# Turning x and v by transfers alone in a graph-network kernel: the transposes of x leave TensorE, a scale factor leaves the first layer norm, and the prologue is laid out anew

## The chip, the cores and the metric

The kernel runs on one core of a Trainium2 chip. The metric is the time of one execution on the device in microseconds (us); the median of three runs before the change is 2247.48 us (2246.62 to 2248.86). The engines of the core are PE (TensorE, with PEld for its weight loads), DVE (VectorE), ACT (ScalarE), POOL (GpSimd) and SP (SyncE), which here only issues transfers.

## The reference, cut to what matters

There are 64 graphs of N = 256 nodes, with D = 256 features in x and an adjacency matrix `adj` of integers. Two layers follow each other, each with a residual and a layer norm:

```
# layer 0: three rounds of message passing, each followed by a GRU cell
A = (adj != 0); h = x
for i in 0..2:
    a = A^T (h W_i)
    r = sigmoid(a Wir + h Whr + b); z = sigmoid(a Wiz + h Whz + b)
    n = tanh(a Win + bi + r * (h Whn + bh))
    h = (1 - z) * n + z * h
x1 = layernorm(x + h)                  # (v - mean) / sqrt(var + 1e-5), v = x + h

# layer 1: graph attention
Wh = x1 W;  s1 = Wh a1;  s2 = Wh a2
e = leaky_relu(s1[:, None] + s2[None, :], 0.2), and -9e15 where adj <= 0
x2 = layernorm(x1 + softmax(e) Wh)
```

## The kernel before

**Tiles.** Two graphs make a pair (NP = 32 pairs, K = 4 tiles of 128 nodes to a pair). Features lie on the partitions wherever they are contracted: `hT` holds h as [128, 2 halves of D, 512 nodes]. x comes from DRAM with nodes on the partitions, and `to_T` (L265) turns it: four 128x128 transposes on PE for each half of D, L269, and a copy out of PSUM by ACT and DVE in turn (L113, L115).

**Precision.** A product of float32 numbers is made of pieces: `upper` (a rounded high part, ACT, L129), `lower` (the rest, L132) and `cross` (L135, DVE). Weights are cut into pieces once, by `cut_weight`. The aggregation with A takes x or h as `hi` and `lo` (L306, L132). For layer 0 `lo` is made on POOL, for the others on DVE.

**Work of one block (p, i): pair p, layer i.** `front` (L291) turns h where needed (`turn`, L275 for i > 0), makes `hi` and `lo` (`split`, `rest`), aggregates (L340: 16 matmuls of 256 columns, eight for each half of D), and cuts h and the aggregate into pieces. `gates` (L357) runs 72 matmuls of 512 columns (L369) in eight products; each product ends with an evacuation by ACT (L374, L376) and one by DVE (L378). Then come sigmoid and tanh on ACT (L387), and products, differences and sums on POOL (L395, L396 in `blend`; L401; L405); the sum that makes the new h is on DVE (L408).

**Attention of a pair** (`attention`, L442). x in its turned form was put away in DRAM (`stash`, xT) and comes back as `vT`; DVE adds h (L451). `halves` splits v's numbers into their two 16-bit halves (ACT L460, DVE L461), `back` turns the halves by two transposing transfers of 256 KB on SP (L469), `join` brings them together as v with nodes on the partitions (ACT L478, DVE L479). `layer_norm` (L410) takes the statistics (L418, L419), rs = (var + eps)^-0.5 on POOL (L422, L423), and scales v on ACT (L430). `project` (L493) multiplies vT by W and the attention vectors, with the mean taken out of the weights; `spread` scales by rs (L502, L504). Scores, mask, maximum and exponentials follow (L512, L516, L525, L527, L530), the transposes of the exponentials (`weights_T`, L540) and their copy (L558), the product with Wh (`combine`, L548), its sum with v (`add`, L554), the second layer norm, and the store.

**Order.** A planner written in the kernel keeps a heap of steps with due times in ticks. `gates` lets the clock tick as it lays out its products, 12 ticks a block; whatever is due is laid out there, and each engine runs its own instructions in this order. Blocks go round as (T, 0), (T-1, 1), (T-2, 2), so three pairs are under way, and a turn of 36 ticks brings in one pair. The front of a block is laid out one block ahead of its gates, at the paces `LOOSE` (2, 3, 4, 6, 7, 8 for turn, split, rest, aggregate, upper and rest of the aggregate) or `CLOSE`. The attention of a pair begins with its third block's end, t; its steps stand at t+5 to t+72.

**Buffers.** x and adj have one buffer each (tags "x" and "adj"), hT four, A three. `wh` holds v's 16-bit halves and later Wh; `sc` holds the turned halves and later the scores; both have one buffer but in the last two pairs. All transfers in the loop are issued by SP, one after another; an issue that waits holds up all that stand behind it.

**Prologue.** w_hh is loaded and turned by PE (`rows_T`, L213) and cut; then w_ih; `fold` (L226) makes W_i w_ih; then come x and the first block's front.

Of the kernel before, what the change touches and what calls it, by code (L numbers as in the profile page):

```python
# [9 lines left out]
F32 = mybir.dt.float32  # L10
F32R = mybir.dt.float32r
U8 = mybir.dt.uint8
U16 = mybir.dt.uint16
I32 = mybir.dt.int32
AF = mybir.ActivationFunctionType
ALU = mybir.AluOpType
# [10 lines left out]
def kernel(  # L27
# [77 lines left out]
    def bank(name):  # L105
        return psum.tile([P, 512], F32, tag="bank", name=name)
# [53 lines left out]

    loaded, loaded_adj = {}, {}

    def load_x(p):
# [9 lines left out]
    def load_rows(src, tags, eng):  # L173

        ts = []
        for tag, (o0, o1) in zip(tags, ((0, 4), (4, 6))):
            t = work.tile([P, C, GN], F32, tag=tag, name=f"rows_{tag}_{o0}")
            v = t.rearrange("p a b -> p (a b)")[:, :(o1 - o0) * D].rearrange("p (o d) -> p o d", d=D)
            eng.dma_start(v, src[o0 * P:o1 * P].rearrange("(o p) d -> p o d", p=P))
            ts.append((o0, o1, v))  # L180
        return ts

    wh_n = load_rows(w_hh, ("hH", "hL"), nc.sync)
    wi_n = load_rows(w_ih, ("aH", "aL"), nc.scalar)
    w_n = []
    for i, tag in enumerate(("wh", "v", "v")):
# [4 lines left out]
        w_n.append(t)  # L191
    load_x(0)
    load_adj(0)
    make_identity(nc, ident)
    nc.gpsimd.memset(half, -0.5)
    nc.gpsimd.memset(neg, NEG_INF)
    nc.gpsimd.dma_start(bi, b_ih.rearrange("(c p) -> p c", p=P))
# [9 lines left out]

    def rows_T(src, use):
        for c in range(C):
            for o0, o1, t in src:  # L210
                pt = bank("pw")
                for o in range(o1 - o0):
                    nc.tensor.transpose(pt[:, o * P:(o + 1) * P], t[:, o, c * P:(c + 1) * P], ident)  # L213
                use(c, o0 * P, o1 * P, pt[:, :(o1 - o0) * P])

    def square_T(src, name):
        pt = bank("pw")
        for e in range(C):
            for d in range(C):
                nc.tensor.transpose(pt[:, (e * C + d) * P:(e * C + d + 1) * P],  # L220
                                    src[:, d, e * P:(e + 1) * P], ident)
        dst = work.tile([P, K, P], F32, tag="hi1", name=name, bufs=1)
        nc.scalar.copy(flat(dst), pt)
        return dst.rearrange("p k n -> p (k n)").rearrange("p (e d) -> p e d", e=C)

    def fold(i, wT, d):  # L226
        for o0, o1 in ((0, 512), (512, O)):
            pt = bank("pw")
            for e in range(C):
                nc.tensor.matmul(pt[:, :o1 - o0], wT[:, e, d * P:(d + 1) * P], wih(e, o0, o1),  # L230
                                 start=(e == 0), stop=(e == C - 1))
            cut_weight([t[:, d, o0:o1] for t in wc[i]], pt[:, :o1 - o0], f"{i}_{d}_{o0}")
# [32 lines left out]
    def to_T(src, dst, d):  # L265
# [4 lines left out]
        after(1, lambda: evacuate(dst[:, d, :], pt))  # L270

    def from_T(hT, d):
        pt = bank("pt")
        for k in range(K):
            nc.tensor.transpose(pt[:, k * P:(k + 1) * P], hT[:, d, k * P:(k + 1) * P], ident)  # L275
        return pt

    def begin(p):

        s = pairs[p] = Pair()  # L280
        s.x, s.adj = loaded.pop(p), loaded_adj.pop(p)
        s.A = work.tile([P, G, C, N], F32R, tag="A", name=f"A_{p}", bufs=3)
        nc.vector.tensor_scalar(s.A, s.adj, 0.0, None, op0=ALU.not_equal)
        s.hT = work.tile([P, C, GN], F32, tag="hT", name=f"hT_{p}", bufs=4)

# [5 lines left out]
    def front(p, i, t, pace):  # L291
# [4 lines left out]
        def turn(d):  # L296
            s = pairs[p]
            if i == 0:
                src[d] = nodes(s.x, d)
                to_T(s.x, s.hT, d)  # L300
            else:
                src[d] = from_T(s.hT, d).rearrange("p (k n) -> p k n", k=K)

        def split(d):
            hi[d] = work.tile([P, K, P], F32R, tag=f"hi{d}", name=f"hi{d}_{nm}", bufs=1)
            nc.scalar.copy(hi[d], src[d])  # L306

        def rest(d):
            lo[d] = work.tile([P, K, P], F32R, tag=f"lo{d}", name=f"lo{d}_{nm}", bufs=1)
            lower(nc.gpsimd if i == 0 else nc.vector, lo[d], src[d], hi[d])  # L310

# [4 lines left out]
        if i == 0:  # L316
            at(t + pace[0][1] + 2, stash)

# [90 lines left out]

    def layer_norm(v, name, t, then=None):  # L410

# [9 lines left out]
        def power():  # L421
            nc.gpsimd.tensor_scalar(rs, mv[:, :, 1], EPS, None, op0=ALU.add)  # L422
            nc.gpsimd.tensor_tensor(rs, rs, half, ALU.pow)  # L423
# [10 lines left out]
        at(t[1], power)  # L434
        at(t[2], shift)
        for k in range(K):
            at(t[3] + k // 2, lambda k=k: apply(k))
        if then:
            at(t[3] + 2, then)
        return rs  # L440

    def attention(p, t):  # L442
# [9 lines left out]

        def halves(d):

            if d == 0:
                s.wh = room("wh", [P, G, C, D], p)
                s.apart = s.wh.rearrange("p g c d -> p (g c d)").bitcast(U16).rearrange(
                    "p (c h n) -> p c h n", c=C, h=2)
            src = s.vT.bitcast(U16).rearrange("p c (n h) -> p c n h", h=2)
            nc.scalar.copy(s.apart[:, d, 0, :], src[:, d, :, 0])  # L460
            nc.vector.tensor_copy(s.apart[:, d, 1, :], src[:, d, :, 1])  # L461

        def back(d):

            if d == 0:
                s.sc = room("sc", [P, K, N], p)
                s.turned = s.sc.rearrange("p k n -> p (k n)").bitcast(U16).rearrange(
                    "p (h k d) -> p h k d", h=2, k=K)
            nc.sync.dma_start_transpose(  # L469
                s.turned.rearrange("p h k d -> p (h k) d")[:, :, d * P:(d + 1) * P],  # L470
                s.apart[:, d].rearrange("p h n -> p (h n)"))

        def join(g):
            if g == 0:
                s.v = room("v", [P, G, C, D], p)
            dst = s.v[:, g].rearrange("p c d -> p (c d)").bitcast(U16).rearrange("p (n h) -> p n h", h=2)
            src = s.turned[:, :, g * C:(g + 1) * C, :].rearrange("p h c d -> p h (c d)")
            nc.scalar.copy(dst[:, :, 0], src[:, 0])  # L478
            nc.vector.tensor_copy(dst[:, :, 1], src[:, 1])  # L479
        for d in range(C):  # L480
            at(t + 22 + d, lambda d=d: halves(d))
            at(t + 23 + d, lambda d=d: back(d))
        for g in range(G):
            at(t + 29 + g, lambda g=g: join(g))
        at(t + 30, lambda: setattr(s, "rs", layer_norm(s.v, f"a_{p}", (t + 31, t + 33, t + 34, t + 49))))

# [45 lines left out]
        for k in range(K):  # L532
            at(t + 47 + k // 2, lambda k=k: exps(k))
        at(t + 52, lambda: nc.vector.reciprocal(s.sm, s.sm))

# [20 lines left out]
        for g in range(G):  # L556
            at(t + 53 + g, lambda g=g: weights_T(g))
            at(t + 54 + g, lambda g=g: nc.vector.tensor_copy(flat(s.sc[:, g * C:(g + 1) * C, :]), pts[g]))  # L558
            at(t + 57 + g, lambda g=g: combine(g))
            at(t + 58 + g, lambda g=g: add(g))  # L560

        def store():
            nc.sync.dma_start(out[p * G:(p + 1) * G].rearrange("g (c p) d -> p g c d", p=P), s.v)
            del pairs[p]
        at(t + 60, lambda: layer_norm(s.v, f"b_{p}", (t + 61, t + 64, t + 66, t + 70), store))


    CLOSE = (5, 5, 5, 7, 8, 8), (6, 6, 7)
    LOOSE = (2, 3, 4, 6, 7, 8), (5, 8, 10)


# [4 lines left out]

    rows_T(wh_n, lambda c, o0, o1, pt: cut_weight([t[:, c, o0:o1] for t in whh], pt, f"h{c}_{o0}"))
    begin(0)
    masking(0)
    load_adj(1)  # L580
    rows_T(wi_n, lambda c, o0, o1, pt: evacuate(wih(c, o0, o1), pt))
    nc.vector.tensor_add(b_sum, bi, bh)
    wT = square_T(w_n[0], "wT_0")
    front(0, 0, clock[0], LOOSE)
    for d in range(C):
        fold(0, wT, d)
        tick(3)
    tick(10)
# [12 lines left out]
    for n, (p, i) in enumerate(blocks):  # L601
        if n + 1 < len(blocks):
            np_, ni = blocks[n + 1]
            if ni == 0:
                after(1, lambda p=np_: begin(p))
            front(np_, ni, clock[0], CLOSE if n and np_ == blocks[n - 1][0] else LOOSE)
            if ni == 0:
                after(7, lambda p=np_: load_x(p + 1))
                after(19, lambda p=np_: masking(p))
                after(20, lambda p=np_: load_adj(p + 1))  # L610
        gates(p, i, (2, 3, 5) if n + 2 >= len(blocks) or blocks[n + 2][0] == p else (4, 5, 10))
        if i == L - 1:
            attention(p, clock[0])
# [32 lines left out]
```

## Time and profile before

| engine | busy us of the span of 2247.1 | share |
|---|---|---|
| PE | 2189.0 | 97% |
| PEld | 1813.6 | 81% |
| DVE | 1728.2 | 77% |
| ACT | 1556.4 | 69% |
| POOL | 1535.2 | 68% |

| group | count | mean ns |
|---|---|---|
| L269 PE, transpose of x, 128x128 | 256 | 272 |
| L132 POOL, `lo` of x, 128x512 | 64 | 1397 |
| L460 ACT, L461 DVE, halves of v, 128x512 uint16 | 64 each | 614, 577 |
| L478 ACT, L479 DVE, join of v, 128x512 uint16 | 64 each | 786, 892 |
| L430 ACT, scaling by the first norm, 128x256 | 128 | 591 |
| L426 DVE, shift of the first norm, 128x4 | 32 | 1171 |
| L469 SP, transposing transfer of 256 KB, issue to landing | 64 | 3.1 us |
| x, adj from DRAM, 512 KB, issue to landing | 32 each | 3.9 us |

Busy time of PE counts an instruction from its start to its modelled end; consecutive matmuls overlap, so that two of 630 ns can start 467 ns apart. A "wait" in the trace is idle time of an engine just before an instruction, with what released it. The chain is followed back from the last instruction, through what released each. Two gate matmuls appear as one row "x2" of the timeline.

### The profile page before, as it was taken

How to read it: one execution, taken by the hardware profiler on the slowest of the kernel's cores; microseconds unless marked ns; L12 is line 12 of the kernel's file. 1: busy time of each engine (PE TensorE's matmuls, PEld its weight loads, DVE VectorE, ACT ScalarE, POOL GpSimd, SP SyncE). 2: the span in 40 equal slices, each digit the busy share in tenths (PEclk: the TensorE clock that was granted, in tenths of full speed). 3: DMA queues.
4: the chain of work that ended last, by engine and by line, in shares of the span. 5: the costliest groups of instructions: out<-in, count | busy, mean ns of one | idle time of the engine just before them, and what ended most of it. 6: DMA issues, size and time to landing. Idle time of an engine off the chain costs nothing.

```text
span 2247.1 us, 31126 instructions
## 1 busy us (share of the span) xinstructions
PE 2189.0 (97%) x10724; PEld 1813.6 (81%) x10724; DVE 1728.2 (77%) x2920; ACT 1556.4 (69%) x2899; POOL 1535.2 (68%) x1084
## 2 busy tenths in 40 slices
PE   7999999999999999999999999999999999999985
PEld 5788888888888888888888888888888888888864
DVE  4667778878778878778878778878778878778875
ACT  4566777677777677777677777677777677777665
POOL 5777667767667767667767667767667767667751
PEclk9999999999999999999999999999999999999997
DMA  3011111111111211112111111111111111111111
GB/s 113 29 38 38 34 42 57 57 48 38 42 43 57 57 47 38 41 45 57 57 48 38 41 45 57 57 48 38 40 46 57 57 48 38 39 47 38 29 38 47
DMA packets 130237, 105.30 MB, mean 47 GB/s; under 512 B 70368, under 2 KB 121824, under 8 KB 130080
## 3 DMA queue, kind: packets, MB, share of 16 engines
q1 hardware_dynamic: 128288, 101.47, 15.4%
q8 instruction: 86, 1.41, 0.3%
q10 hardware_dynamic: 1616, 1.57, 0.2%
q14 instruction: 71, 0.58, 0.1%
q0 software_dynamic: 176, 0.27, 0.1%
HBM read 52.96 MB, written 33.55 MB: 39 GB/s over the span
## 4 chain that ended last, share of the span: by engine, by line
PE 85%; POOL 10%; ACT 1%; DVE 1%; DMA 1%; issue 1%; POOLq 0%; SPq 0%; ACTq 0%; DVEq 0%
PE pga L369 42%; PE pgb L369 21%; PE pa L340 7%; PE po L548 5%; PE pwh L493 5%; POOL t L396 3%; PE pt L275 3%; POOL lo L132 2%; POOL t L395 2%; PE pt L540 1%; POOL n L405 1%; POOL n L401 1%; PE pt L269 1%; POOL rs_b L423 1%; DMA adj<-in_adj_dram 1%
## 5 line engine op out<-in xcount | busy, mean ns | idle before, releaser
L395 POOL TENSOR_TENSOR t<-hT,n 128x512 f32<-128x512 f32 x192 | 288.4, 1502 | 540.1 <-ACT n L387 540.0
L369 PE MATMUL pga<-hH,whhH_whh 128*128 128x512 f32 x1152 | 388.8, 418 | 0.0
L369 PE MATMUL pgb<-hD,whhD_whh 128*128 128x512 f32 x1152 | 362.0, 395 | 0.8 <-DVE hD L135 0.8
L369 PE MATMUL pga<-hL,whhL_whh 128*128 128x512 f32 x1152 | 362.3, 395 | 0.0
L405 POOL TENSOR_TENSOR n<-n,t 128x512 f32<-128x512 f32 x192 | 283.8, 1478 | 57.8 <-DVE t L378 45.5
L396 POOL TENSOR_TENSOR t<-t,z 128x512 f32<-128x512 f32 x192 | 280.6, 1461 | 15.1
L374 ACT ACTIVATE r<-pga 128x512 f32<-128x512 f32 x192 | 114.5, 596 | 235.6 <-PE pga L369 193.0
L369 PEld LDWEIGHTS pgb<-hD,whhD_whh 128*128 128x128 f32 x1152 | 216.3, 188 | 53.3 <-DVE hD L135 1.3
L369 PEld LDWEIGHTS pga<-hL,whhL_whh 128*128 128x128 f32 x1152 | 216.3, 188 | 51.6 <-POOL hL L132 0.2
L401 POOL TENSOR_TENSOR n<-n,r 128x512 f32<-128x512 f32 x192 | 252.8, 1317 | 0.8 <-DVE n L378 0.7
L132 POOL TENSOR_TENSOR hL<-hT,hH 128x1024 fp32r<-128x1024 f32 x96 | 243.8, 2540 | 8.9 <-ACT hH L129 8.9
L376 ACT ACTIVATE n<-pga,bh 128x512 f32<-128x512 f32 x192 | 131.6, 685 | 154.3 <-PE pga L369 154.0
L378 DVE SCALAR_TENSOR_TENSOR r<-pgb,r 128x512 f32<-128x512 f32 x192 | 131.7, 686 | 135.1 <-ACT r L374 75.2
L369 PEld LDWEIGHTS pga<-hH,whhH_whh 128*128 128x128 f32 x1152 | 196.0, 189 | 24.1
L340 PE MATMUL pa<-A,lo 128*128 128x256 f32 x768 | 195.9, 287 | 12.5 <-POOL lo L132 12.4
L340 PE MATMUL pa<-A,hi 128*128 128x256 f32 x768 | 196.5, 287 | 0.0
L378 DVE SCALAR_TENSOR_TENSOR n<-pgb,n 128x512 f32<-128x512 f32 x192 | 131.5, 685 | 67.5 <-ACT n L376 64.5
L387 ACT ACTIVATE z<-z,b_sum 128x512 f32<-128x512 f32 x192 | 141.6, 738 | 43.1 <-DVE z L378 42.7
L340 PEld LDWEIGHTS pa<-A,lo 128*128 128x128 f32 x768 | 146.9, 191 | 27.2 <-POOL lo L132 21.6
L378 DVE SCALAR_TENSOR_TENSOR t<-pgb,t 128x512 f32<-128x512 f32 x192 | 131.7, 686 | 38.5 <-ACT t L374 36.4
L135 DVE SCALAR_TENSOR_TENSOR hD<-hH,hT 128x1024 fp32r<-128x1024 f32 x96 | 156.5, 1630 | 0.0
L340 PEld LDWEIGHTS pa<-A,hi 128*128 128x128 f32 x768 | 146.8, 191 | 7.2
(136 smaller groups left out, 5495.6 us busy)
## 6 DMA issues: line engine op xcount, KB each, us to landing
x<-in_x_dram SPq DMA_DIRECT2D x32, 512.0 KB, 3.9
adj<-in_adj_dram SPq DMA_DIRECT2D x32, 512.0 KB, 3.9
xT<-hT SPq DMA_DIRECT2D x32, 512.0 KB, 2.6
vT<-xT SPq DMA_DIRECT2D x32, 512.0 KB, 3.3
out_dram<-v SPq DMA_DIRECT2D x32, 512.0 KB, 2.9
sc<-wh SPq DMA_TRANSPOSE x64, 3.1
w_n<-in_L_gnn_weight_dram ACTq DMA_DIRECT2D x3, 256.0 KB, 10.3
rows_aH<-in_L_gnn_w_ih_dram ACTq DMA_DIRECT2D x1, 512.0 KB, 6.1
```

The source lines that it names most:

```text
L132: eng.tensor_sub(dst, src, hi.bitcast(F32))
L135: nc.vector.scalar_tensor_tensor(dst, hi.bitcast(F32), 1.0 + U, src, op0=ALU.mult, op1=ALU.subtract)
L340: nc.tensor.matmul(pt[:, g * N:(g + 1) * N], h[:, g * C + c, :], s.A[:, g, c, :], start=(n == 0), stop=(n == len(todo) - 1))
L369: nc.tensor.matmul(pt, w[:, d, o * P:(o + 1) * P], m[:, d, :], start=n in (0, ends + 1), stop=n in (ends, len(todo) - 1))
L374: nc.scalar.activation(dst, a, AF.Copy, scale=1.0 + U)
L376: nc.scalar.activation(dst, a, AF.Identity, scale=1.0 + U, bias=bias)
L378: nc.vector.scalar_tensor_tensor(dst, b, -1.0 / U, dst, op0=ALU.mult, op1=ALU.add)
L387: nc.scalar.activation(dst, dst, func, bias=bias)
L395: nc.gpsimd.tensor_sub(t, h, n)
L396: nc.gpsimd.tensor_mul(t, t, z)
L401: after(2, lambda r=r, n=n: nc.gpsimd.tensor_mul(n, n, r))
L405: after(1, lambda n=n, t=t: nc.gpsimd.tensor_add(n, n, t))
```

## The change

**x.** From the sixth pair on (p >= FROM = L + 2 = 5) x is no longer turned by PE. `x_turned` reads x from DRAM as 16-bit numbers, 512 rows of 512, by one transposing transfer into the buffer of x; even partitions then hold low halves of the features' float32 numbers and odd ones high halves. `second` brings the halves together on their partitions by four transfers with a partition step of two, into the buffer of adj. `x_joined` interleaves the halves with two copies on ACT and two on DVE, and so fills hT. x itself is loaded after that, as the aggregation needs it, and adj after the join.

**v.** The split on ACT and DVE (`halves`) goes: the transposing transfers read vT directly (`turn`), and four transfers (`second`) bring the halves together. The join stays.

**First norm.** v is no longer scaled by rs and shifted. The second norm doesn't see a common factor or shift, apart from eps: its eps becomes eps * (var + eps), and the sum of exponentials is multiplied by rs ahead of its reciprocal.

**Order.** The front of layer 0 gets the pace `FIRST`, with `split` and `rest` two ticks earlier; A is made a tick later; the steps of the attention from `weights_T` on move up by two or three ticks.

**Prologue.** x is loaded first; pair 0's front runs beside the turning of the weights; its `lo` is made on DVE; the weight pieces come in another order; a first sigmoid loads ACT's table early.

The diff, cut to its core:

```diff
+    FROM = L + 2
...
+    load_x(0)
     wh_n = load_rows(w_hh, ("hH", "hL"), nc.sync)
+    load_adj(0)
     wi_n = load_rows(w_ih, ("aH", "aL"), nc.scalar)
...
-    load_x(0)
-    load_adj(0)
...
+    nc.scalar.activation(warm, half, AF.Sigmoid)
...
+    def put_together(dst, hi, lo):
+        dst = dst.bitcast(U16).rearrange("p (n h) -> p n h", h=2)
+        nc.scalar.copy(dst[:, :, 1], hi)
+        nc.vector.tensor_copy(dst[:, :, 0], lo)
+    def x_turned(p):
+        first = io.tile([P, G, C, D], F32, tag="x", name=f"first_{p}")
+        t1 = first.rearrange("p g c d -> p (g c d)").bitcast(U16).rearrange("p (q n) -> p q n", n=GN)
+        nc.sync.dma_start_transpose(t1, x[p * G:(p + 1) * G].rearrange("g n d -> (g n) d").bitcast(U16))
+        def second():
+            t2 = io.tile([P, G, C, N], I32, tag="adj", name=f"second_{p}")
...
+            for h in range(2):
+                for b in range(2):
+                    nc.sync.dma_start(s.halves[b * 64:b * 64 + 64, h], t1b[h::2, b])
+        return second
+    def x_joined(p):
+        begin(p)
+        s = pairs[p]
+        for d in range(C):
+            put_together(s.hT[:, d, :], s.halves[:, 1, d, :], s.halves[:, 0, d, :])
...
             if i == 0:
-                src[d] = nodes(s.x, d)
-                to_T(s.x, s.hT, d)
+                if p < FROM:
+                    to_T(s.x, s.hT, d)
...
-            lower(nc.gpsimd if i == 0 else nc.vector, lo[d], src[d], hi[d])
+            lower(nc.gpsimd if i == 0 and p else nc.vector, lo[d], src[d], hi[d])
...
-            nc.gpsimd.tensor_scalar(rs, mv[:, :, 1], EPS, None, op0=ALU.add)
+            if eps is None:
+                nc.gpsimd.tensor_scalar(rs, mv[:, :, 1], EPS, None, op0=ALU.add)
+                nc.gpsimd.tensor_scalar(nm, rs, EPS, None, op0=ALU.mult)
+            else:
+                nc.gpsimd.tensor_add(rs, mv[:, :, 1], eps)
             nc.gpsimd.tensor_tensor(rs, rs, half, ALU.pow)
...
-            nc.scalar.copy(s.apart[:, d, 0, :], src[:, d, :, 0])
-            nc.vector.tensor_copy(s.apart[:, d, 1, :], src[:, d, :, 1])
...
             nc.sync.dma_start_transpose(
-                s.turned.rearrange("p h k d -> p (h k) d")[:, :, d * P:(d + 1) * P],
-                s.apart[:, d].rearrange("p h n -> p (h n)"))
+                s.first.rearrange("p k b d -> p (k b) d")[:, :, d * P:(d + 1) * P],
+                s.vT[:, d, :].bitcast(U16))
+        def second():
...
+            for h in range(2):
+                for b in range(2):
+                    nc.sync.dma_start(s.halves[b * 64:b * 64 + 64, h], s.first[h::2, :, b])
...
-            at(t + 22 + d, lambda d=d: halves(d))
-            at(t + 23 + d, lambda d=d: back(d))
+            at(t + 20 + d, lambda d=d: turn(d))
+        at(t + 24, second)
         for g in range(G):
-            at(t + 29 + g, lambda g=g: join(g))
+            at(t + 28 + g, lambda g=g: join(g))
...
-        at(t + 52, lambda: nc.vector.reciprocal(s.sm, s.sm))
+            nc.vector.tensor_mul(s.sm, s.sm, s.rs)
+            nc.vector.reciprocal(s.sm, s.sm)
...
-            at(t + 53 + g, lambda g=g: weights_T(g))
-            at(t + 54 + g, lambda g=g: nc.vector.tensor_copy(flat(s.sc[:, g * C:(g + 1) * C, :]), pts[g]))
-            at(t + 57 + g, lambda g=g: combine(g))
-            at(t + 58 + g, lambda g=g: add(g))
+            at(t + 51 + g, lambda g=g: weights_T(g))
+            at(t + 52 + g, lambda g=g: nc.vector.tensor_copy(flat(s.sc[:, g * C:(g + 1) * C, :]), pts[g]))
+            at(t + 54 + g, lambda g=g: combine(g))
+            at(t + 55 + g, lambda g=g: add(g))
...
+    FIRST = (2, 1, 2, 6, 7, 8), (5, 8, 10)
...
-                after(1, lambda p=np_: begin(p))
...
-                after(7, lambda p=np_: load_x(p + 1))
-                after(19, lambda p=np_: masking(p))
-                after(20, lambda p=np_: load_adj(p + 1))
+                if np_ < FROM:
+                    after(1, lambda p=np_: begin(p))
+                after(1, lambda p=np_: take_x(p))
+                after(2, lambda p=np_: ones(p))
+                nxt = np_ + 1
+                if nxt < FROM:
+                    after(7, lambda p=nxt: load_x(p))
+                elif nxt < NP:
+                    later = {}
+                    after(22, lambda p=nxt, d=later: d.update(f=x_turned(p)))
+                    after(26, lambda d=later: d["f"]())
+                    after(30, lambda p=nxt: x_joined(p))
+                    after(31, lambda p=nxt: load_x(p))
+                early = 3 if np_ + 1 < FROM else 0
+                after(19 - early, lambda p=np_: masking(p))
+                after(20 - early if nxt < FROM else 32, lambda p=nxt: load_adj(p))
```

## The prediction

> **What bounds the kernel now.** I read first the table of stretches over four periods of the steady state (a pair of graphs enters every 67.44 us; columns: length, then busy us of PE, PEld, DVE, ACT, POOL, clock, DMA share, GB/s), since the page's shares average over stages.
>
> ```profile
> 742.65:810.10 67.45, 67.15 (x334) 55.87 (x333) 53.30 (x91) 48.31 (x91) 47.39 (x34) 1.00 0.17 48
> 810.10:877.54 67.44, 67.13 (x334) 55.85 (x333) 53.32 (x91) 48.28 (x91) 47.53 (x33) 1.00 0.16 48
> ```
>
> PE is idle 0.30 us of 67.44. The other engines have 14 us or more to spare, the DMA engines over 80%. But a busy PE need not be a PE at its pace, as its matmuls overlap; so I read its timeline next, start to start:
>
> ```profile
> 1015.57 0.63 PE L369 MATMUL pgb<-hD,whhD_whh 128*128 128x512 f32 x2
> 1016.03 0.63 PE L369 MATMUL pgb<-aD,wc2D_wc 128*128 128x512 f32 x2
> 1016.50 0.60 PE L269 MATMUL pt<-ident,x 128*128 128x128 f32 x4
> 1016.85 0.71 PE L369 MATMUL pga<-hH,whhH_whh 128*128 128x512 f32 x2
> 1017.40 0.63 PE L369 MATMUL pga<-hL,whhL_whh 128*128 128x512 f32 x2
> ```
>
> Two gate matmuls start every 0.467 us, the same all through the period: this is PE's pace and there is no hidden wait in it. From 1016.50 to 1017.40 stand four transposes of x and two gate matmuls: 0.90 - 0.467 = 0.433 us for four transposes (0.109 each, not the 272 ns of the row, most of which overlaps the neighbours). A pair needs eight, 0.87 us.
>
> The 0.30 us of idling is one wait, seen in the list of waits (us in total, times, longest) and in the chain:
>
> ```profile
> PE pa L340 <- POOL lo L132: 12.4, 28, 4.3
> ```
>
> ```profile
> 1018.84 0.23 POOL rs_b L422
> ...
> 1020.19 1.51 POOL lo L132
> 1021.70 1.45 POOL t L395
> ...
> 1024.59 1.26 POOL lo L132
> 1025.89 1.10 PE pa L340 x7
> ```
>
> The aggregation of layer 0 waits for the second low half of x, which stands on POOL behind the power of the second layer norm and behind one `blend`. Of 12.4 us in 28 waits one is 4.3 (prologue); the other 27 are (12.4 - 4.3)/27 = 0.30 each. POOL's part of the chain (10% of the page) comes in through this one door.
>
> **What the skill says.** "Perfetto Trace Analysis", Identifying the Most-Contended Engine: matmul busy share is a poor measure of how near PE is to its limit, because matmuls are pipelined; hence the spacing above, which agrees in both directions (a 272 ns transpose costs 109). "Advanced Engine Details and Errata", X-Bar Transpose (TRN2): transpose transfers are about as fast as ordinary ones. The trace agrees: 256 KB transposed land in 3.1 us, 512 KB plain in 2.6 to 3.9. "DMA: Bandwidth & Descriptors", Two DMAs through the same engine are not ordered: a transfer that reads what another wrote must wait for its completion. So transpose and gather follow each other in full, and SP stands still in between.
>
> **The change, part by part.** A tick is a twelfth of a block, 67.44/36 = 1.87 us; B is the tick at which a pair's layer 0 is laid out, and its predecessor's attention starts at t = B+12.
>
> *x by transfers, from pair 5 on (27 pairs).* Removed: 27 x 0.87 = 23.5 us of PE, on the path; one ACT copy (588 ns) and one DVE copy (683) a pair. Added: two ACT copies of 128x512 uint16 (786 each, the row of v's join) and two on DVE (892). They lie in slack.
>
> The transfers have deadlines instead. On SP the reload of xT waits for the previous attention's products on PE (t+38, which is B+14); then comes the transpose of 512 KB from DRAM, a form that the trace doesn't have. Value: twice the issue of the 256 KB one and its landing, 2 x 1.24 + 3.1 = 5.6 us. Low end 2.0 (524 KB at the 261 GB/s that "DMA: Bandwidth & Descriptors", Latency and other measured facts, gives). High end 21 (16 blocks at the 1309 ns for a 128x128 block in "VectorE: DVE Perf Modes", The three transpose paths; the trace's eight blocks in 3.1 us speak against it). Four gathers of 128 KB follow: 4 x 0.37 issue + 3.9 = 5.4 us (as much again, if 1 KB pieces are slow). The join is due at B+30, 16 ticks or 30 us later: 11 needed, 26 or, at both high ends, 32. The central case has 19 us of margin.
>
> Behind the waiting SP stand the load of x (needed at B+37; it waits only for the gathers, so it can land near B+22), that of adj (it waits for the join, lands about 6 us after B+30, needed at B+38, 15 us after), and v's transposes.
>
> *v by transfers.* Removed: 2 x 614 ns of ACT and 2 x 577 of DVE a pair, and what they waited for: the ACT copies idled 116.0 us in all until PE's `combine` freed the buffer. That wait passes to SP. From there (B+31) the second transpose is issued after 1.24 us and lands 3.1 later, 4.3 us; the gathers take 5.4 (10.8 if their 512-byte pieces are slow): 9.7 (15.1) against the 9 ticks or 16.9 us up to the join at B+40. Hidden.
>
> *Factor of the first norm.* ACT loses 4 x 591 ns a pair, DVE one 1.17; DVE gains one small product, POOL 0.23. With everything ACT goes from 48.3 to about 45.7 us, DVE from 53.3 to 52.3, POOL from 47.4 to 47.6, each of 66.3: no new bound, and nothing gained on the path but in the tail.
>
> *Order.* In the new program order both low halves of x stand ahead of the power and the blend on POOL, so at 1018.8 in the picture above they would start 1.4 and 2.8 us earlier relative to the aggregation: the 0.30 us wait goes, 27 x 0.30 = 8.1 us. The attention's last steps move up 2 or 3 ticks: `combine` now follows its DVE copy by 2 ticks (3.7 us) instead of 3. Before, that copy ended about 3.3 us after the transposes; in the new PE order about 4.6 us of matmuls lie between. 1.3 us of margin: it should just fit.
>
> *Prologue.* PE idles 4.34 us until POOL has the first low half (25 to 27.5 us, behind weight pieces and a late x). Now x is loaded first, and its low half is made on DVE at once; a table load of 1.28 us leaves the path too. What takes over is DVE's weight cutting and `hL` on POOL. I take 5 us (1 to 10).
>
> *Tail, the 66 us after the last gate matmul at 2181.3.* The chain there holds 1.75 us of the removed ACT scalings (2219.8 to 2221.7), 0.5 of the halves copy, and a wait of 3.06 for a transpose that began at 2193.9, although its vT was ready at 2185.2. The gathers add about 4 us to each of the last pairs, but start 5 to 8 earlier. I take 4 us of gain (-4 to 12: much of this stretch is idle, and its order changes).
>
> Sum: 23.5 + 8.1 + 5 + 4 = 40.6; 2247.5 - 40.6 = 2207 us, a period of 67.44 - 0.87 - 0.30 = 66.27.
>
> **Rivals.** *New waits eat a part:* the `combine` margin of 1.3 us, or DVE's joins standing ahead of an evacuation, give PE a new wait of some 0.3 us a pair, and the old one stays or moves. For it: program order moved in four places, with margins of 1 to 2 us. Against: ACT and DVE get emptier. Then 23.5 - 8 from the steady state and 6 at the ends: 2226. *A transfer comes late:* if the transpose from DRAM takes 30 us, the gathers are over at 35, ACT and DVE stop for 5 us in every pair, and PE soon after: 27 x 5 - 40 = +95, 2342 us. For it: a form never seen here, and SP passes every delay on to all that is behind. Against: the 256 KB row. *The loop through POOL and ACT sets the pace, not PE:* then freed PE time turns to idling, and only the ends gain, 2238. For it: POOL's 10% of the chain. Against: 0.30 us of idling.
>
> **How the numbers follow.** Forecast 0.70, eaten 0.20, late transfer 0.06, loop 0.04. At the ends the unknown costs leave 5 + 8 = 13 us more to gain, which gives the lower bound, 2194, and 4 + 8 = 12 less; with half of the 8 us of the wait kept that is 2223, and I go on to 2226, the centre of the second case. Left out are the late transfer, the loop and the upper half of the second case. Faster by over 0.2%: all cases but the late transfer and a sliver of the loop, 0.92; same 0.02; slower 0.06.
>
> **What would show it.** Right: a period of about 66.3 us; x transposes by PE in the first five pairs only; no wait of PE's for `lo`; the transpose from DRAM landing within 10 us; the first gate matmul some 5 us before 29.5. Wrong: a wait of ACT or DVE for `second` or for `sc`, or of PE for `sc` at `combine`; a period of 66.9 or more; PE idle by over 0.5 us a period.

## The result and the profile after

The changed kernel takes 2168.85 us (median of four executions, 2168.29 to 2170.38) against 2247.36 (2246.62 to 2248.86) beside it: a ratio of 0.9651, 95% interval 0.9634 to 0.9668. That is 78.5 us less, where 40.6 were forecast, and below the range of 2194 to 2226.

The stretches of the changed kernel over two of its periods (same columns as before):

```profile
740.40:805.53 65.13, 65.13 (x325) 55.17 (x324) 53.80 (x89) 46.68 (x86) 49.47 (x35) 1.00 0.30 73
805.53:870.66 65.13, 65.13 (x325) 55.19 (x324) 53.83 (x89) 46.62 (x86) 49.43 (x35) 1.00 0.29 73
```

PE no longer idles at all, and between 300 and 2000 us its list of waits is empty. But the period fell by 2.31 us (67.44 to 65.13), twice the 1.17 of the sum. The second surprise stands in PE's timeline (start, duration; two gate matmuls to a row):

```profile
1021.50 0.62 PE L412 MATMUL pga<-hH,whhH_whh 128*128 128x512 f32 x2
1021.95 0.62 PE L412 MATMUL pga<-hL,whhL_whh 128*128 128x512 f32 x2
1022.40 0.62 PE L412 MATMUL pga<-aH,wc1H_wc 128*128 128x512 f32 x2
1022.86 0.62 PE L412 MATMUL pga<-aL,wc1L_wc 128*128 128x512 f32 x2
```

Two now start every 0.453 us, not every 0.467. Averaged over all starts deep in a row of gate matmuls (the twelfth and later, 300 to 2000 us), a matmul of 512 columns follows the last after 226.7 ns instead of 233.3, though neither these matmuls nor the clock (1.00 in both) were touched. With 216 of them a pair that alone is worth well over 20 us.

The chain of the changed kernel is PE's almost throughout; POOL's 10% are gone:

```profile
PE 95%; DVE 2%; POOL 1%; ACT 1%; DMA 0%; issue 0%; POOLq 0%; ACTq 0%; SPq 0%; DVEq 0%
```

The new transfers, from the list of issues (KB each, median us from issue to landing; `second` are x's gathers, sc<-wh those of v) and from the view of L289, the transpose of x from DRAM (in 980 to 1120 us; over all 27 of them the landing takes 4.9 to 7.2 us, median 5.4):

```profile
sc<-wh SPq DMA_DIRECT2D x128, 128.0 KB, 3.4
second<-first SPq DMA_DIRECT2D x108, 128.0 KB, 3.0
wh<-vT SPq DMA_TRANSPOSE x64, 3.2
```

```profile
L289 SPq DMA_TRANSPOSE first<-in_x_dram x2: 2882/3270/3658, 1005.1 to 1070.2; - x2
DMA to landing us min/median/max: 5.0/5.4/5.9
```

The first gate matmul starts at 21.97 us (29.49 before), and from the end of the last one to the end of the span pass 60.9 us (65.8 before).

### The profile page after: what moved, and what is told of

Read it like the earlier page. It is cut to its first block, busy times and chain, and to the rows that moved or that the text cites. A ratio compares the mean times of both kernels' runs of the same rounds, so it can differ in the third digit from the quotient of the medians.

```text
span 2166.5 us, 30928 instructions
## 1 busy us (share of the span) xinstructions
PE 2124.7 (98%) x10508; PEld 1790.7 (83%) x10508; DVE 1735.2 (80%) x2885; ACT 1497.1 (69%) x2734; POOL 1593.0 (74%) x1114
## 4 chain that ended last, share of the span: by engine, by line
PE 95%; DVE 2%; POOL 1%; ACT 1%; DMA 0%; issue 0%; POOLq 0%; ACTq 0%; SPq 0%; DVEq 0%
PE pga L412 48%; PE pgb L412 24%; PE pa L383 8%; PE po L601 5%; PE pwh L541 5%; PE pt L311 3%; PE pt L593 1%; PE s L560 1%; DMA rows_hH<-in_L_gnn_w_hh_dram 0%; PE pw L236 0%; POOL t L438 0%; POOL wc2L_wc L147 0%; POOL t L439 0%; DVE v L607 0%; DVE cut L133 0%
## 5 line engine op out<-in xcount | busy, mean ns | idle before, releaser
L438 POOL TENSOR_TENSOR t<-hT,n 128x512 f32<-128x512 f32 x192 | 273.0, 1422 | 392.0 <-ACT n L430 391.8
L412 PE MATMUL pga<-hH,whhH_whh 128*128 128x512 f32 x1152 | 375.7, 407 | 0.0
L412 PE MATMUL pga<-hL,whhL_whh 128*128 128x512 f32 x1152 | 357.6, 392 | 1.0 <-POOL hL L133 1.0
L448 POOL TENSOR_TENSOR n<-n,t 128x512 f32<-128x512 f32 x192 | 274.9, 1432 | 77.8 <-DVE t L421 67.5
L439 POOL TENSOR_TENSOR t<-t,z 128x512 f32<-128x512 f32 x192 | 303.4, 1580 | 15.0
L383 PE MATMUL pa<-A,hi 128*128 128x256 f32 x768 | 202.3, 297 | 0.2 <-DVE A L322 0.2
L136 DVE SCALAR_TENSOR_TENSOR hD<-hH,hT 128x1024 fp32r<-128x1024 f32 x96 | 190.5, 1985 | 0.0
L451 DVE TENSOR_TENSOR hT<-t,n 128x512 f32<-128x512 f32 x192 | 165.6, 863 | 4.3 <-POOL t L439 4.3
L417 ACT ACTIVATE t<-pga 128x512 f32<-128x512 f32 x192 | 114.6, 597 | 68.1 <-PE pga L412 68.1
L430 ACT ACTIVATE r<-r,b_sum 128x512 f32<-128x512 f32 x192 | 139.2, 725 | 23.1 <-DVE r L421 22.6
```

What stands on the lines that cost most here:

```text
L136: nc.vector.scalar_tensor_tensor(dst, hi.bitcast(F32), 1.0 + U, src, op0=ALU.mult, op1=ALU.subtract)
L383: nc.tensor.matmul(pt[:, g * N:(g + 1) * N], h[:, g * C + c, :], s.A[:, g, c, :], start=(n == 0), stop=(n == len(todo) - 1))
L412: nc.tensor.matmul(pt, w[:, d, o * P:(o + 1) * P], m[:, d, :], start=n in (0, ends + 1), stop=n in (ends, len(todo) - 1))
L417: nc.scalar.activation(dst, a, AF.Copy, scale=1.0 + U)
L430: nc.scalar.activation(dst, dst, func, bias=bias)
L438: nc.gpsimd.tensor_sub(t, h, n)
```

## The experiments

Each kernel ran beside the one before the change; the medians of that one lay between 2247.4 and 2248.2 throughout. Periods are start to start of the same matmul one pair later. Single profiles of kernels with the same prologue differ in it: the first gate matmul starts at 21.8 to 23.3 us, and the next block's first one follows 30.8 to 32.6 us later.

### Addresses: what set the matmuls' pace

The change puts a small tile, `warm`, into the constants' pool. With its size rounded up it takes 32 bytes a partition, so the tiles of all pools behind the constants lie 32 bytes higher, the gate matmuls' moving tiles (h and the aggregate, in pieces) among them; the weights, which stand ahead of it, don't move. My theory was that the moving tiles had been 32 bytes off a multiple of 64 and now were on one. An unused tile that also rounds up to 32 bytes tells; one, two or three of them in the kernel before (32, 64, 96 bytes), or one in the changed kernel:

```diff
     neg = const.tile([P, 1], F32, name="neg")
+    pad0 = const.tile([P, 1], F32, name="pad0")
```

> The kernel before with one unused tile of 32 bytes a partition put in the constants' pool, so that every tile of the later pools lies 32 bytes higher, as it does in the changed kernel. Theory A (addresses): the changed kernel's gate matmuls start every 226.7 ns instead of 233.3 because their moving tiles now begin on a multiple of 64 bytes; this kernel should show the same 226.7 ns, and 27 or more pairs x 216 gate matmuls x about 4.6 ns, 32 us, less: 2212 to 2220 us. Theory B (less traffic of ACT, DVE and POOL beside PE is what speeds up the matmuls): 233.3 ns, and 2247 us. Theory C (the new order of PE's instructions): 2247 us too.

Measured: 2229.44 us (ratio 0.9913, 0.9898 to 0.9928), 226.7 ns, a period of 66.89. An unused tile alone makes the old kernel 0.9% faster; less traffic and another order (theories B and C) are out. The gain is 19 us, not 32. PE's timeline has the new pace, and its list of waits has a longer wait than the 0.30 us of before:

```profile
1004.38 0.61 PE L370 MATMUL pga<-aH,wc2H_wc 128*128 128x512 f32 x2
1004.84 0.62 PE L370 MATMUL pga<-aL,wc2L_wc 128*128 128x512 f32 x2
1005.29 0.62 PE L370 MATMUL pgb<-hD,whhD_whh 128*128 128x512 f32 x2
```

```profile
PE pa L341 <- POOL lo L132: 11.5, 25, 0.5
```

11.5/25 = 0.46 us a pair: the wait for the low half ate part of it (see the order, below).

> The kernel before with 64 unused bytes instead of 32: the addresses move, but their remainder modulo 64 is that of before. Theory A: 233.3 ns and 2247 us, no change. If any move of the addresses, or the smaller room left, were what counts, this would be as fast as the kernel with 32 bytes. Theories B and C: 2247 us.

Measured: 2248.2 us (ratio 1.0, 0.9991 to 1.0008), 233.3 ns. Moving the tiles is not enough; where they land counts.

> The changed kernel with 32 more unused bytes, so that the tiles of the later pools are again 32 bytes off a multiple of 64, as before the change. Theory A: gate matmuls every 233.3 ns, a period of about 66.1 us as the prediction summed it up, 2169 + 32 = 2201 us, which is what the change is worth without the addresses. Theories B and C: 226.7 ns and 2169 us.

Here the pad stands in the changed kernel. Measured: 2197.36 us (ratio 0.9768, 0.9752 to 0.9784), 233.3 ns, a period of 66.05. So 28.5 of the 78.5 us come from 32 bytes, and the change proper is worth 50. That the gate matmuls are what the bytes act on can be summed from the two traces: the times from one gate matmul's start to that of the next, where nothing stands between, come to 47.94 us a period with the pad and 47.03 without (means of 18 periods), 0.9 of the 0.92 us by which the periods differ. PE's timeline with the pad has the old 0.467 again:

```profile
1058.23 0.63 PE L413 MATMUL pga<-hL,whhL_whh 128*128 128x512 f32 x2
1058.69 0.63 PE L413 MATMUL pga<-aH,wc1H_wc 128*128 128x512 f32 x2
1059.16 0.63 PE L413 MATMUL pga<-aL,wc1L_wc 128*128 128x512 f32 x2
```

Next, which operand? In the first of the two following kernels a 32-byte tile stands in the work pool ahead of the load of w_ih, so only hH and hL keep their address; in the second, one ahead of the weights and one behind `neg`.

```diff
+    work.tile([P, 1], F32, tag="padw", name="padw", bufs=1)
     wi_n = load_rows(w_ih, ("aH", "aL"), nc.scalar)
```

> The changed kernel with 32 unused bytes between hL and aH, so that hH and hL begin on a multiple of 64 bytes and hD, aH, aL and aD 32 bytes off it. Theory A1 (each matmul's own moving operand counts): in long rows of gate matmuls those that move hH and hL start 226.7 ns apart, those that move hD, aH, aL and aD 233.3; two thirds of 0.91 us a period more, 65.74 us, and 2169 + 20 = 2189 us. Theory A2 (it is the writers, or the tiles as a whole, that slow PE down): one spacing for all kinds, somewhere between.

Measured: 2193.89 us, a period of 65.95, a mean of 232.5 ns. Both theories fell as stated. By the matmul that the spacing follows, the kinds don't separate cleanly: hH 232.0 and hL 229.9 although their address hadn't changed, hD 232.3, aH 233, aL 234.6. So a matmul's spacing isn't set by its own moving tile alone.

> The changed kernel with all weights 32 bytes off a multiple of 64 (they were on it before and after), and the moving tiles still on it. Theory: the weights are loaded beside the matmuls (a load lies beside the matmul before it), so their address doesn't count: 226.7 ns and 2169 us. Rival: weights count as much as the moving operand: slower by 10 to 30 us.

Measured: 2198.17 us (ratio 0.9778, 0.9764 to 0.9793), 233.3 ns, a period of 66.05, just as with the moving tiles moved. My theory fell: the weights' address counts as much. Either operand off is slow; so what if both are? Only the pad ahead of the weights, which moves everything by 32:

> The changed kernel with weights and moving tiles both 32 bytes off a multiple of 64. If the two operands' addresses count relative to each other: 226.7 ns and 2169 us, as with both on a multiple. [...]If one being off is enough: 233.3 ns and 2198 us.

Measured: 2170.36 us, 226.7 ns, a period of 65.13. With both 32 bytes off a multiple of 64 the pace is the fast one:

```profile
1050.09 0.62 PE L413 MATMUL pga<-hH,whhH_whh 128*128 128x512 f32 x2
1050.54 0.62 PE L413 MATMUL pga<-hL,whhL_whh 128*128 128x512 f32 x2
1051.00 0.61 PE L413 MATMUL pga<-aH,wc2H_wc 128*128 128x512 f32 x2
```

Had each operand's 32 bytes cost its own 6.6 ns, both would have given 240. It is not alignment: it is the distance between the moving tile and the weight. Four more kernels change the distance (96 bytes of pads in the kernel before; 128 in the changed kernel, which there also begins the transfers two pairs earlier; two constants of 32 bytes moved from behind the weights to ahead of them; and 2304 bytes of constants moved so). The third of them:

```diff
+    bi = const.tile([P, OC], F32, name="bi")
+    bh = const.tile([P, OC], F32, name="bh")
     whh = pieces(const, [P, C, O], "whh", "whh")
...
-    bi = const.tile([P, OC], F32, name="bi")
-    bh = const.tile([P, OC], F32, name="bh")
```

> The kernel before with 96 unused bytes: the moving tiles begin on a multiple of 64 bytes that is not one of 128 (in the one with 32 bytes they began on a multiple of 128). If 64 bytes are what counts: as with 32 bytes, 226.7 ns and 2229 us. If it takes a multiple of 128: 233.3 ns and 2248 us, or something between.

Measured: 2229.4 us, the time of the 32-byte pad, though 228.9 ns deep in the rows. The waits don't hide a difference, for there is none: summed over a period the starts of gate matmuls take 46.80 us here, 46.81 with the 32-byte pad and 47.51 without a pad, since the first starts of each row come quicker here. The spacing deep in a row is not the whole cost.

> The changed kernel with x turned by transfers from the fourth pair on, and 128 unused bytes, so that the moving tiles begin on a multiple of 512 bytes and not only of 128. If 64 bytes are all that counts: 226.7 ns and 2167 us. If more alignment speeds the moving operand up further, a spacing under 226 ns and less.

Measured: 2190.37 us, 232.6 ns. More alignment made it slower, and the hoped-for best version fell with it.

> The changed kernel with two small constants placed ahead of the weights instead of behind them: the weights lie 64 bytes higher, all moving tiles where they were, so the distance between them is a multiple of 256 plus 192. If 64 less is like 64 more: 228 to 230 ns, and 2169 + 10 = 2179 us or less. If only the remainder modulo 64 counts: 226.7 and 2169.

Measured: 2200.32 us, 233.3 ns, a period of 66.13: 64 bytes less is not like 64 more, and the remainder modulo 64 alone is out. Here only the weights and a few constants moved; the moving tiles, and so what is written into them, kept the addresses that they have in the fast kernel.

```profile
988.58 0.63 PE L412 MATMUL pga<-hH,whhH_whh 128*128 128x512 f32 x2
989.04 0.63 PE L412 MATMUL pga<-hL,whhL_whh 128*128 128x512 f32 x2
989.51 0.63 PE L412 MATMUL pgb<-hD,whhD_whh 128*128 128x512 f32 x2
```

> The changed kernel with 2304 bytes of constants placed ahead of the weights: the distance becomes a multiple of 512 bytes, where it was one of 256. If 256 is the period: 226.7 ns and 2169 us. If 512 does better: under 226 ns, and under 2165 us; if worse, over 2175.

Measured: 2168.72 us, 226.7 ns.

The distances can be counted from the tiles' sizes, each rounded up to 32 bytes (no run prints an address; the runs agree with the count). From the first weight tile to hH lie, before the change, 12 x 6144 + 2080 + 4 x 32 + 512 + 2 x 32 + 2 x 4096 = 84704 bytes = 330 x 256 + 224; with `warm` 84736 = 331 x 256. The slices that the gate matmuls use and the steps between their tiles are multiples of 256, so in all kernels but the one that splits h from a, one remainder holds for every pair of operands (the summed starts are those from gate matmul to gate matmul, as above):

| distance modulo 256 | kernels | ns, start to start deep in a row | summed starts of a period before the change, us | summed starts of a period, changed kernel, us | period of the changed kernel |
|---|---|---|---|---|---|
| 0 | changed; 32-byte pad before the change; both on 32; 2304 moved | 226.7 | 46.81 | 47.03 | 65.13 (2304 moved: 65.09) |
| 32 | 64-byte pad before; 32-byte pad after; weights on 32 | 233.3 | 47.55 | 47.94 | 66.05 |
| 64 | 96-byte pad before | 228.9 | 46.80 | | |
| 128 | 128-byte pad after | 232.6 | | 47.72 | 65.84 |
| 192 | two constants moved | 233.3 | | 48.02 | 66.13 |
| 224 | before | 233.3 | 47.51 | | |

The table fits a period of 256 bytes; 0 was met at an odd multiple of 256 and at a multiple of 512. "TensorE: Matmul & The Clock Gate", Step-by-step: what each phase is for, states that PE reads the moving operand and the next weights through two independent ports and that loading weights doesn't steal bandwidth from the running matmul. For these matmuls the measurement differs: the two streams are not indifferent to each other's addresses. Why is not shown by any run. The same page, Back-to-back issue gap, gives 512/2.4 + 2.5 = 216 ns as the isolated gap of a 512-column matmul and about 131 ns as the sustained one; the traces here have 226.7 at best.

### Order: what the wait for the low half cost

The list of waits had 0.30 us a pair. The timeline of before around one such wait shows more (start, duration, idle time in brackets):

```profile
957.86 0.28 PE L340 MATMUL pa<-A,hi 128*128 128x256 f32 x1
958.44 0.39 PE L340 MATMUL pa<-A,lo 128*128 128x256 f32 x1 [0.30 <-POOL lo L132]
958.67 0.28 PE L340 MATMUL pa<-A,hi 128*128 128x256 f32 x1
958.78 0.28 PE L340 MATMUL pa<-A,lo 128*128 128x256 f32 x1
```

These matmuls start 0.12 us apart when nothing is waited for. Here the gaps are 0.58 and 0.23: (584 - 120) + (223 - 120) = 567 ns lost. The list counts from the *end* of the matmul ahead, 0.28 us after its start, but a pipelined PE would have started the next one long before that end.

```diff
-    FIRST = (2, 1, 2, 6, 7, 8), (5, 8, 10)
+    FIRST = (2, 3, 4, 6, 7, 8), (5, 8, 10)
```

> The changed kernel with the first layer's low halves of x back at the ticks they had before (pace LOOSE in place of FIRST), so that on POOL they stand behind the power and the blend again. The trace of before, looked at again, shows that where the list of waits has 0.30 us of idling a pair, the starts of the two aggregation matmuls lie 584 and 223 ns apart instead of 120 each, 0.57 us lost, since the list counts from the end of a matmul that overlaps its neighbours. Theory (the prediction's step, with this size): the wait comes back at about 0.3 us and costs 0.57 us in each of 27 or more pairs, 15 to 17 us: 2185 us, period 65.7. With the prediction's own size, 27 x 0.30 = 8.1 us: 2177, period 65.4. Rival (the wait went because v's and the norm's work left ACT and DVE, not because of the order): 2169.

Measured: 2200.65 us (ratio 0.9786, 0.977 to 0.9803), a period of 66.22, and the wait back, longer than ever, with POOL back in the chain:

```profile
PE pa L383 <- POOL lo L133: 21.5, 26, 0.8
```

```profile
PE 76%; POOL 17%; ACT 3%; DVE 2%; DMA 2%; issue 1%; SPq 0%; POOLq 0%; ACTq 0%; DVEq 0%
```

32 us, twice what I expected of it. The other way round, in the kernel before, the order alone:

```diff
+    FIRST = (2, 2, 3, 6, 7, 8), (5, 8, 10)
...
-            front(np_, ni, clock[0], CLOSE if n and np_ == blocks[n - 1][0] else LOOSE)
+            front(np_, ni, clock[0], CLOSE if n and np_ == blocks[n - 1][0] else LOOSE if ni else FIRST)
```

> The kernel before with one edit of order: the low halves of x for the first layer come one tick earlier (FIRST = 2, 2, 3 for the first layer), so on POOL the first stands ahead of the power and the second ahead of the blend. Theory: the wait for the low half goes, and with it 0.57 us a pair by the starts of the two aggregation matmuls (584 and 223 ns in place of 120 each): a period of 66.87 us, 2247.4 - 28 x 0.57 = 2231 us. With the prediction's 0.30 a pair: 67.14 and 2239. If the order is worth what its undoing in the changed kernel cost, 1.09 a pair: 66.35 and 2217.

Measured: 2233.17 us (ratio 0.9935, 0.992 to 0.995), a period of 66.87, exactly the 0.57; no wait is left:

```profile
740.00:806.87 66.87, 66.87 (x334) 55.87 (x333) 52.96 (x91) 48.17 (x91) 48.33 (x34) 1.00 0.16 48
```

> The kernel before with that order and 32 unused bytes, x still turned on PE. Theory: without the wait the addresses bring their whole 0.91 us a pair: a period of 65.96 us and 2231 - 28 = 2203 us. If the 19 us that the padding alone brought are its full worth here, 66.3 and 2212.

Measured: 2212.93 us, a period of 66.17, 226.7 ns, no wait. So the wait's cost is no constant. With PE's own work at 66.87, 66.17 and 65.13 us a period, the old order gives periods of 67.44, 66.89 and 66.22, a loss of 0.57, 0.72 and 1.09 us. With a faster PE more of the chain runs through POOL (10% of it in the kernel before, 17% with the pad); the low halves' new place removed the wait. The pad brought 0.70 here, where 32 bytes bring 0.92 in the changed kernel. The rows account for it: the sum of gate starts falls by 0.71 (47.52 to 46.81). Behind x's transposes the matmuls start unevenly, 224 to 236 ns apart and 231 on the mean, for some eight starts before they settle at 226.7, and in the old order `combine` breaks two more rows. So turning x on PE costs more at the fast pace.

### The other parts

PE turns x for all pairs, the transfers run on, and their halves are not used:

```diff
-            put_together(s.hT[:, d, :], s.halves[:, 1, d, :], s.halves[:, 0, d, :])
...
-                if p < FROM:
-                    to_T(s.x, s.hT, d)
+                to_T(s.x, s.hT, d)
```

> The changed kernel, with x turned by PE for every pair (8 transposes, one ACT and one DVE copy a pair more); the transfers are still made, but their halves are not brought together. The term of 23.5 us by itself: if eight transposes cost 0.87 us of PE's time a pair, 27 x 0.87 = 23.5 us more, 2192 us. If part of the excess gain lay in the transposes (each costing more than its 0.109 us, by a switch between transposes and gate matmuls), 27 x 2.0 = 54 us more, 2223 us. If PE had room for them, 2169 us.

Measured: 2197.02 us, a period of 66.09. 0.96 us a pair, 27 x 0.96 = 25.9 us; the other 2 of the 28 fit a prologue that ended some 3 us later in its profile.

The scaling and shift of the first norm done again (`apply` and `shift` laid out, no product in `divide`):

> The changed kernel with the scaling of the first layer norm done again (four ACT passes of 512, a shift, no product in the softmax). Theory: ACT has some 18 us of slack in a period of 65.1, so the period stays at 65.13 and only the tail gets longer, by 1.75 us: about 2171 us. Rival (less ACT work is part of what speeds up the steady state): a period of 65.3 or more, 2175 us or more.

Measured: 2173.43 us (2171.84 to 2173.63), a period of 65.13; the tail grows from 60.9 to 62.9 us, and the first gate matmul of its profile is 0.7 us later. So 4.6 us are lost at the ends, of which the profile places 2.0 in the tail. ACT has 1.8 us more work in a period, and the period doesn't change:

```profile
740.00:805.13 65.13, 65.13 (x327) 55.15 (x325) 54.91 (x90) 48.45 (x90) 49.37 (x34) 1.00 0.29 73
```

The transpose from DRAM issued three times:

```diff
+        for _ in range(3):
             nc.sync.dma_start_transpose(t1, x[p * G:(p + 1) * G].rearrange("g n d -> (g n) d").bitcast(U16))
```

> The changed kernel with the 512 KB transpose of x from DRAM issued three times in a row for every pair from the fifth on. One takes 3.0 us of SP and lands 5.4 us after its issue, so the gathers and the join come 6 to 11 us later. The prediction gave the transfers 19 us of room. Theory (room enough): 2169 us, no change. Rival (the room is smaller, since SP hands its delay on to v's transposes and the loads of x and adj): waits of ACT or DVE for the halves, and 27 x 1 us or more, 2196 us or over.

Measured: 2168.73 us. The DMA engines are busier by a quarter (0.30 to 0.37 of this stretch), the period stays:

```profile
1050.00:1115.00 65.00, 65.00 (x326) 55.01 (x325) 53.66 (x89) 46.64 (x85) 49.30 (x35) 1.00 0.37 90
```

x and adj of the first pair loaded after the weights again:

> The changed kernel with x and adj of the first pair loaded after the weights, as before the change; all else of the new prologue stays. If the early load is what brings the first gate matmul from 29.5 to 22 us, it starts at 27 us or later here and the time is 5 us longer, 2174 us. If the low half on DVE and the table load did most of it, 2169 to 2171 us.

Measured: 2174.97 us (ratio 0.9677, 0.9662 to 0.9691); the first gate matmul starts at 27.66 us. In its list of waits PE's first one is

```profile
PE pt L275 <- DMA x<-in_x_dram: 13.0, 1, 13.0
```

against 6.2 us in the changed kernel. The early load is worth 6.1 us, most of the prologue's gain; the low half on DVE and the early table load were not tried alone.

FROM = 3 in place of L + 2 = 5:

> The changed kernel with x turned by transfers from the fourth pair on instead of the sixth (pairs 3 and 4 too). By the 0.96 us that turning x on PE costs a pair, 1.9 us less: 2167 us. If the early pairs have waits elsewhere that hide it, no change, 2169 us; if the transfers come too early for the prologue's loads, slower.

Measured: 2167.28 us (2166.18 to 2168.95), 1.6 us less, as two more pairs without transposes should bring; its runs overlap the changed kernel's own, so the gain itself is not shown.

## Why the prediction was wrong

The direction was right. The size was not, and the runs take it apart. Four kernels form a path: the one before (period 67.44), that with the new order of the low halves (66.87), the changed kernel at the old pace, with a pad (66.05), and the changed kernel (65.13). The steps are 0.57 + 0.82 + 0.92 = 2.31 us. The middle step holds all the rest of the change; no run undoes v's transfers alone, and that they gain nothing on the path rests on PE's empty list of waits. The ends are read from single profiles, so that the sum meets the measured time within 1 us is in part luck.

| term | forecast us | measured us | from |
|---|---|---|---|
| x off PE, 27 pairs | 23.5 | 22 | 27 x 0.82 (66.87 to 66.05); 26 at the fast pace (27 x 0.96) |
| wait for the low half | 8.1 | 15 | 2248.04 - 2233.17 |
| prologue | 5 | 7.5 | first gate matmul 29.49 to 21.97; 6 to 8 over all profiles |
| tail | 4 | 4.9 | 65.8 to 60.9; 2.0 of it the norm's scaling, the rest not tried alone |
| pace of the gate matmuls | none | 28.5 | 2197.36 - 2168.85 |
| sum | 40.6 | 78 | 78.5 measured |

*The step that failed* was "Two gate matmuls start every 0.467 us, the same all through the period: this is PE's pace and there is no hidden wait in it." The spacing was read correctly, but a regular spacing was taken for the engine's floor. It was a pace that held for one set of addresses, and the change's new tile moved them: 226.7 ns for 233.3, 28.5 us, for a term put at nothing. In the prologue I priced `warm` as a table load and overlooked that it is also a tile ahead of all later pools. No wait and no busy share showed it; the one hint was the new constant in the diff. That its 32 bytes brought the distance from 224 to 256 was luck, as nobody placed it for that. At the old pace (the run with one pad more) the change takes 2197.36 us, inside the range and 10 below the forecast.

*A mis-sized term* was also the wait, "27 x 0.30 = 8.1 us": the mechanism and the cause (POOL's order) were right, but idle time in the list is not the loss of a pipelined engine, which was 0.57 by the starts, and would have become 1.09 with the old order kept.

*What held.* The eight transposes were worth 0.82 to 0.96 us (forecast 0.87). The transfers stay hidden: 5.4 us for the transpose from DRAM (forecast 5.6), 3.0 and 3.4 for the gathers (taken at 3.9), though each gather takes 0.6 us to issue and not 0.37, and three transposes in place of one cost nothing. "The trace agrees" was too much, as it set 256 KB transposed against 512 KB plain: at 512 KB from DRAM the transpose lands after 5.4 us, the plain load after 3.9. POOL has 49.4 us of work a period where 47.6 was forecast, in part because the norm's new small product takes 0.92 us and not 0.23; it costs PE nothing. `combine` gave PE no new wait: the first rival ("New waits eat a part") did not come, nor did the late transfer. The third ("The loop through POOL and ACT sets the pace") was wrong for this kernel but nearer than its 0.04 said: without the new order that loop would have taken back 32 us. The first norm's scaling was worth nothing in the period, as said. The prologue gained 2.5 us more than forecast, inside its span of 1 to 10.

## What to carry to other kernels

Price every new tile in a diff twice: for its work, and for the addresses of all that is allocated after it; here, with PE as the bound, an unused tile of the right size was worth 0.9 to 1.3%, and two kernels that differ by it can't be compared term by term until one is padded. A wait of a pipelined engine is sized by the starts around it, not by the idle time in the list. When an edit frees the bounding engine, ask what wait will grow in its place: the order of POOL's two low halves was worth 15 us alone, and 32 with the rest of the change.

## What the hardware showed

- Matmuls of 512 columns (f32 in the profile), each with its own weight load, start 226.7 ns apart deep in a row when the moving tile lies a multiple of 256 bytes (odd multiples and multiples of 512 were tried) from the weight in the partition, 228.9 at 64 more, and 232.6 to 233.3 at 32, 128, 192 and 224 more. Over a period 64 more is as good as 0 (46.80 and 46.81 us). Either operand's address shifts it; both shifted by the same 32 bytes doesn't.
- Aggregation matmuls of 256 columns start 120 ns apart in both kernels; their operands were shifted together.
- A transpose of 512 KB from DRAM takes SP about 3 us to issue and lands 4.9 to 7.2 us after the issue (median 5.4; a plain load of 512 KB 3.9); issued three times in a row each lands after 4.1 to 7.1 (median 4.6).
